# A gather pipeline paced by TensorE: pairs of indirect DMAs wait for products two groups in front and for their own group's

## The chip, the cores and the metric

The kernel runs on one core of one Trainium2 chip. The metric is the device time of one execution in microseconds, taken without the profiler; the kernel before has a median of 1033.82 us over 3 runs (1021.22 to 1034.26). A profile is a separate execution that the hardware profiler records.

## The reference

One message-passing layer of a graph network, with a residual and two layer norms. There are N = 6250 nodes with H = 128 features, E = 100000 edges sorted by destination, and 4 attributes per edge.

```python
msg_in = concatenate([x[src], x[dst], edge_attr])        # E x 260
h = silu(msg_in @ mW1 + mb1)                             # E x 128
messages = h @ mW2 + mb2
aggregated = segment_sum(messages, dst, N)               # N x 128
u = silu(concatenate([x, aggregated]) @ uW1 + ub1)
updated = u @ uW2 + ub2
x = layernorm(x + layer_norm(x + updated))
```

## The kernel before

**Tiling.** Edges are taken in tiles of 128 and in groups of 8 tiles (`G = 8`), so there are 98 groups (`NG`); the last one has 6 tiles. Since the first product is linear, it is split: `x[src] @ W1a` is a lookup in a table `tab_a` (one row of 128 floats per node, kept in DRAM), `x[dst] @ W1b + mb1` comes from a second table `tab_b`, and the attributes are multiplied directly. A first stage makes both tables: 13 batches of up to four node tiles are transposed and multiplied (L321, L328), copied (L344 for `tab_a`) and written to DRAM.

**One group g** passes through these steps:

- `fetch(g)` (L176 to L186): up to 8 indirect DMAs on GpSimd (POOL), one per tile, each gathering 128 rows of 512 bytes into `rows[g]`. Groups 0 to 4 (`RAW = 5`) gather rows of `x` itself, since the table isn't ready yet; from group 5 on they gather rows of `tab_a`.
- `load(g)` (L453): on the SyncE queue, the destinations (`near`), 80 rows of `tab_b` that cover the group's destinations (`mv`), and the attributes.
- `matrices(g)` (L464): two comparisons on VectorE (L468, L478) that make the 0/1 matrices "edge belongs to destination row", one for each direction.
- `before_rows(g)` (L493): 8 products on TensorE, `pre` (L500), which spread the destination rows and attributes over the edges. For a raw group, the gathered rows are transposed (L489, L491) and multiplied in as well (L502).
- `hidden(g)` (L507): VectorE adds the gathered rows and `pre` (L515), ScalarE applies SiLU into `h` (L516). Raw groups skip the add (L512).
- `sums(g)` (L518): one transpose (L522) and 8 products (L524) on TensorE sum `h` over the edges of each of 80 destinations, and VectorE adds the result into the batch's accumulator at an offset from a register (`add`, L545).

**Nodes.** Every 8 groups a batch of four node tiles is complete, for g = 8, 16, ..., 88, 94 and 97. `node_stage` (L627) then spreads its work over three groups: `node_u` (L562, L569, L570, L572) after `sums(8m)`, `node_y` (L578, L580, L582) one group later, `node_z` and `node_o` (L588 to L622) after a further group. The next batch's node loads, transposes and `tab_b` products (L328) are placed around the same groups.

**Order.** The order on each engine is the order in which the program writes the instructions; a framework only inserts semaphore waits for data and for buffers. In iteration g of the main loop (L652) the order is `fetch(g + 4)`, `load(g + 3)`, `hidden(g)`, `matrices(g + 2)`, `before_rows(g + 1)`, `sums(g)`, `add(g)`, node work. So TensorE has pre(g), sums(g-1), pre(g+1), sums(g) in turn. POOL has nothing but gathers after the first stage. The rows' pool has 6 buffers (`AHEAD + 2`), so the first gather of a group waits until the group six before has been read (for table groups, by L516); the other seven have no wait on a compute engine. A gather also waits for an older gather that used the same DMA semaphore.

Of the kernel before, what the change touches and what calls it, by code (L numbers as in the profile page):

```python
# [24 lines left out]
def kernel(  # L25
# [18 lines left out]
    nc = tc.nc  # L44
# [5 lines left out]
    G = 8  # L50
# [3 lines left out]
    W = 80  # L54
# [6 lines left out]
    RAW = 5  # L61
    NM = 4
# [23 lines left out]
    def tiles_of(g):  # L86
        return min(G, TI - g * G)
# [16 lines left out]
    start = ExitStack()  # L104
    first = start.enter_context(tc.tile_pool(name="first", bufs=1, side="right"))

    def wide():
        return ps.tile([P, G, P], F32, name="pre")

    def narrow():  # L110
        return ps1.tile([P, 2 * P], F32, name="pt")
# [60 lines left out]
    tab_b = dram.tile([NW, H], F32, name="tab_b")  # L172
    ea_d = dram.tile([ED, NG * GE], F32, name="ea_d")
    rows, bases, near = {}, {}, {}

    def fetch(g):  # L176
        if g >= NG:
            return
        rows[g] = gath.tile([P, G, H], F32, name="ga")
        for i in range(tiles_of(g)):  # L180
            nc.gpsimd.indirect_dma_start(  # L181
                out=rows[g][:, i, :],
                out_offset=None,
                in_=x if g < RAW else tab_a[:, :],
                in_offset=bass.IndirectOffsetOnAxis(ap=src_i[:, g, i : i + 1], axis=0),
            )  # L186

    for g in range(RAW - 1):
        fetch(g)
# [6 lines left out]
        ceil_i, pattern=[[BN * P, NB + 1], [0, G]], base=BN * P - W, channel_multiplier=0  # L196
    )
    fetch(RAW - 1)

    b1 = bcast("b1", mb1)  # L200
# [146 lines left out]
    def turned_first(k):  # L347
        pt = wide()
        if k < 2:
            turned_x(k, pt, node, name="xT", bufs=3)  # L350
        else:
            turned_x(k, pt, first, name="xT", bufs=2)
        return pt

    pt = {0: turned_first(0)}
# [25 lines left out]
    mv = []  # L381
# [80 lines left out]
    oh, pre, xg = {}, {}, {}  # L462
# [30 lines left out]
    def before_rows(g):  # L493
        if g >= NG:
            return
        raw = g < RAW
        pre[g] = wide()
        st = stbuf[g % NST].rearrange("k (i c) -> k i c", i=G)
        for i in range(tiles_of(g)):
            nc.tensor.matmul(pre[g][:, i, :], st[:, i, :], mv[g % NM], start=True, stop=not raw)  # L500
            if raw:
                nc.tensor.matmul(  # L502
                    pre[g][:, i, :], xg[g][:, i, :], w1[:, 0, :], start=False, stop=True
                )
        xg.pop(g, None)
# [12 lines left out]
    def sums(g):  # L518
        n = tiles_of(g)
        h, o = hbuf[g % 2], oh.pop(g)  # L520
        pt = narrow()
        nc.tensor.transpose(pt[0:1, P : P + W], deg_g[:, g : g + 1], ident[:W, :W])  # L522
        for i in range(n):
            nc.tensor.matmul(pt[:, :W], h[:, i, :], o[:, i, :], start=i == 0, stop=i == n - 1)  # L524
        return pt

    acc, deg = {}, {}
# [57 lines left out]
    def inverse(*parts):  # L585
        r = node.tile([P, 2, 2 * BN], F32, name="r")
        lo, hi = parts[0][0], parts[-1][1]
        nc.scalar.activation(r[:, 0, lo:hi], var[:, lo:hi, 1], AF.Sqrt, bias=eps)  # L588
        nc.vector.reciprocal(r[:, 0, lo:hi], r[:, 0, lo:hi])
        nc.vector.scalar_tensor_tensor(  # L590
            r[:, 1, lo:hi], var[:, lo:hi, 0], -1.0, r[:, 0, lo:hi], op0=OP.mult, op1=OP.mult
        )
        return r

    def scaled(to, v, r, lo, n):
        for i in range(n):
            nc.scalar.activation(  # L597
                to[:, i, :],
                v[:, i, :],
                AF.Identity,  # L600
                bias=r[:, 1, lo + i : lo + i + 1],
                scale=r[:, 0, lo + i : lo + i + 1],
            )
# [11 lines left out]
    def node_o(k, r):  # L615
        i0, n = batches[k]
        o = node.tile([P, BN, H], F32, name="o")
        scaled(o, z_sb.pop(k), r, BN, n)
        m = min(i0 + n, nf) - i0
        if m > 0:  # L620
            nc.sync.dma_start(
                out[i0 * P : (i0 + m) * P].rearrange("(i p) f -> p i f", p=P), o[:, :m]  # L622
            )
        if i0 + n > nf:
            nc.scalar.dma_start(out[nf * P :], o[: N - nf * P, nf - i0, :])
# [26 lines left out]
    for g in range(NG):  # L652
        if g == 2:
            weights()
        if g == 5:
            merged()
        if g == 6:
            checks(*lists)
            source_lists(1, SK)
            start.close()  # L660
        for c in range(1, NC):
            if g == max(1, c * EC // GE - 8):
                attributes(c)
            if g == max(1, c * EC // GE - 8) + 1:
                attribute_rows(c)
        if g + AHEAD >= RAW:
            fetch(g + AHEAD)
        if g < RAW:
            if g + 1 < RAW:
                turned_rows(g + 1)  # L670
            before_rows(g)
        load(g + LEAD)
        hidden(g)
        matrices(g + 2)
        if g + 1 >= RAW:
            before_rows(g + 1)
        if g == NG - 1:
            node_x(NB - 1)
        add(g, sums(g))
        node_stage(g)  # L680
    k = NB - 1
    n = batches[k][1]
# [6 lines left out]
    node_o(k - 1, r)  # L689
    r = inverse((BN, BN + n))  # L690
    node_o(k, r)
    edges.close()
    ub2_b, g_b, b_b = late["ub2"], late["g"], late["b"]

# [100 lines left out]
    with tc.If(bad > 0):  # L795
        with tc.tile_pool(name="all", bufs=1) as whole:
# [11 lines left out]
            with tc.tile_pool(name="turned", bufs=2, space=PSUM) as turned:  # L808
                for i in range(NT):
                    pt = turned.tile([P, P], F32, name="pt")  # L810
# [142 lines left out]
```

## Time and profile before

| | |
|---|---|
| Median of 3 runs (lowest, highest) | 1033.82 us (1021.22, 1034.26) |
| Profiled execution, and its span | 1463.32 us, 1461.5 us |
| Mean granted TensorE clock in it | 0.561 |
| First gather from `tab_a` (group 5) starts | 93.1 us |
| First gather of group 11 starts | 176.2 us |
| Last gather ends | 1392.6 us |
| DMA over the span | 110.01 MB, 75 GB/s mean |

The profiled execution is 41% longer than the median of the runs. PE is TensorE, PEld its weight load, DVE VectorE, ACT ScalarE, POOL GpSimd, SP SyncE. In a row of groups the columns are line, engine, operation, output and inputs, count, then busy time, mean ns of one, and the idle time of the engine just before, with what ended most of it. A row of the timeline has start, duration, engine, line, operation and count, and in brackets the idle time before it and its releaser. "remote" stands for a wait whose releaser the profile doesn't show, and "issue" for idle time in which the engine waited for nothing that the profile shows.

### The profile page before, as it was taken

The page shows a single profiled execution, that of the slowest core. Times are in us where ns is not written, and L with a number is a line of the kernel's source. Part 1 is how long each engine was busy: PE and PEld are TensorE (multiplying, and loading weights), DVE is VectorE, ACT ScalarE, POOL GpSimd, SP SyncE. Part 2 cuts the span into 40 slices and gives each one's busy share as a digit, 9 for nine tenths or more (in the row PEclk, how much of TensorE's full clock was granted, in tenths as well). Part 3 has the DMA queues.
Part 4 walks back from the last instruction along what each step waited for, and adds up shares of the span by engine and source line. Part 5 has one row for each costly group of instructions (what it writes and reads, how often), then busy time and mean ns, then how long its engine had stood idle before and what let it go on. Part 6 is the DMA issues. An engine that isn't in the chain of part 4 may idle for free.

```text
span 1461.5 us, 12138 instructions
## 1 busy us (share of the span) xinstructions
PE 885.3 (61%) x3858; PEld 777.7 (53%) x3858; DVE 451.3 (31%) x936; ACT 238.8 (16%) x338; POOL 739.3 (51%) x792
## 2 busy tenths in 40 slices
PE   2355766466456747554764764766764764764794
PEld 2355755464455645443763663664653763663683
DVE  0032332322322422412522422422422422422443
ACT  0010112111111201201201301211201201201213
POOL 7334555464554654564564565465564565465400
PEclk9987756556555555555555555555555555555555
DMA  6243313122222222221321321331331321322200
GB/s 165 61 117 92 94 58 87 54 83 63 78 79 61 84 68 77 74 77 41 96 84 47 100 81 51 87 92 52 93 92 46 91 86 52 88 65 64 85 26 19
DMA packets 83074, 110.01 MB, mean 75 GB/s; under 512 B 21084, under 2 KB 62160, under 8 KB 83002
## 3 DMA queue, kind: packets, MB, share of 16 engines
q1 hardware_dynamic: 54178, 55.97, 13.2%
q0 software_dynamic: 25024, 51.30, 12.6%
q10 hardware_dynamic: 3800, 1.88, 0.5%
q8 instruction: 33, 0.54, 0.1%
q14 instruction: 39, 0.32, 0.1%
HBM read 97.81 MB, written 11.27 MB: 75 GB/s over the span
## 4 chain that ended last, share of the span: by engine, by line
another core or an unknown queue 37%; PE 25%; DVE 16%; issue 12%; ACT 5%; DVEq 2%; DMA 1%; POOL 1%; ACTq 0%; SPq 0%
PE pt L524 12%; PE pre L500 4%; DVE ga L515 4%; DVE st L468 4%; ACT h L516 3%; DVE oh L478 2%; PE pn L569 2%; PE pn L570 2%; ACT pn L597 2%; DVE bn L556 1%; PE pn L328 1%; DVE var L557 1%; PE pre L328 1%; DVEq L515 1%
## 5 line engine op out<-in xcount | busy, mean ns | idle before, releaser
L181 POOL DMA_INDIRECT ga<-tab_a,src_i x742 | 699.9, 943 | 638.5 <-ACT h L516 372.1
L524 PE MATMUL pt<-oh,h 128*128 128x80 f32 x1564 | 348.1, 415 | 174.6 <-ACT h L516 156.8
L524 PEld LDWEIGHTS pt<-oh,h 128*128 128x128 f32 x1564 | 332.8, 323 | 194.9 <-ACT h L516 172.2
L500 PE MATMUL pre<-mv,st 84*128 84x128 f32 x1564 | 351.0, 409 | 23.1 <-issue 22.1
L500 PEld LDWEIGHTS pre<-mv,st 84*128 84x128 f32 x1564 | 332.4, 318 | 28.3 <-issue 27.0
L545 DVE TENSOR_TENSOR acc<-acc,pt 128x80 f32 x98 | 23.4, 238 | 733.1 <-remote 504.1
L516 ACT ACTIVATE h<-ga 128x1024 f32<-128x1024 f32 (+1 forms) x93 | 98.1, 1055 | 726.2 <-DVE ga L515 541.1
L522 PE MATMUL pt<-ident,deg_g 80*1 80x80 f32 x98 | 30.9, 315 | 191.6 <-DVE deg L545 191.6
L468 DVE TENSOR_SCALAR_CACHE_REDUCE st<-near,base_p 80x1024 f32<-80x1024 int32 x98 | 124.3, 1269 | 7.1 <-issue 5.2
L515 DVE TENSOR_TENSOR ga<-ga,pre 128x1024 f32<-128x1024 f32 (+1 forms) x93 | 113.2, 1217 | 26.8 <-issue 22.0
L522 PEld LDWEIGHTS pt<-ident,deg_g 80*1 80x1 f32 x98 | 10.7, 109 | 199.7 <-DVE deg L545 199.6
L478 DVE TENSOR_TENSOR oh<-w_row,rel 128x640 f32<-128x640 f32 x98 | 79.8, 814 | 0.0
L569 PE MATMUL pn<-acc,wc 128*128 128x512 f32 (+2 forms) x26 | 24.3, 1037 | 89.2 <-DVE acc L545 89.2
L569 PEld LDWEIGHTS pn<-acc,wc 128*128 128x128 f32 x26 | 6.9, 312 | 106.2 <-DVE acc L545 104.1
L181 POOL DMA_INDIRECT ga<-in_x_dram,src_i x40 | 37.9, 947 | 14.2 <-issue 11.7
L321 PE MATMUL pre<-ident,x 128*128 128x128 f32 x49 | 13.8, 434 | 43.6 <-issue 26.6
L321 PEld LDWEIGHTS pre<-ident,x 128*128 128x128 f32 x49 | 8.6, 216 | 47.5 <-issue 26.9
L328 PEld LDWEIGHTS pn<-w,xT 128*128 128x128 f32 x98 | 20.2, 305 | 25.6 <-ACT uT L572 22.7
L597 ACT ACTIVATE pn<-y,r 128x128 f32<-128x128 f32 x49 | 22.6, 461 | 65.6 <-DVE r L590 59.0
L344 DVE COPY ta<-pre 128x512 f32<-128x512 f32 (+2 forms) x13 | 8.6, 661 | 75.9 <-remote 42.3
L337 DVE TENSOR_TENSOR o<-pn,b 128x512 f32<-128x512 f32 (+2 forms) x13 | 8.6, 661 | 74.3 <-PE pn L328 63.1
L536 ACT COPY acc<-acc 128x256 f32<-128x256 f32 (+1 forms) x12 | 5.0, 413 | 159.8 <-DVE acc L545 155.8
(117 smaller groups left out, 532.8 us busy)
## 6 DMA issues: line engine op xcount, KB each, us to landing
near<-in_dst_dram SPq DMA_DIRECT2D x97, 320.0 KB
ga<-tab_a,src_i POOLq DMA_INDIRECT x742
mv<-tab_b SPq DMA_DIRECT2D x98, 40.0 KB
x<-in_x_dram SPq DMA_DIRECT2D x14, 256.0 KB
tab_a<-ta SPq DMA_DIRECT2D x11, 256.0 KB
tab_b<-o SPq DMA_DIRECT2D x11, 256.0 KB
out_dram<-o SPq DMA_DIRECT2D x11, 256.0 KB
st<-ea_d SPq DMA_DIRECT2D x98, 16.0 KB
```

What stands on the lines that cost most here:

```text
L181: nc.gpsimd.indirect_dma_start(out=rows[g][:, i, :], out_offset=None, in_=x if g < RAW else tab_a[:, :], in_offset=bass.IndirectOffsetOnAx ...
L328: nc.tensor.matmul(pm[:, i, :], xT[k][:, i * P : (i + 1) * P], w1[:, part, :], start=True, stop=True)
L468: nc.vector.tensor_scalar(stbuf[g % NST][:W], near.pop(g), base_p[:W, g : g + 1], 0.0, op0=OP.is_equal, op1=OP.add, accum_out=deg_g[:, g : ...
L478: nc.vector.tensor_tensor(oh[g][:, :n], w_row[:, None, :].to_broadcast([P, n, W]), rel[:, g, :n, None].to_broadcast([P, n, W]), op=OP.is_e ...
L500: nc.tensor.matmul(pre[g][:, i, :], st[:, i, :], mv[g % NM], start=True, stop=not raw)
L515: nc.vector.tensor_add(s[:, :n], s[:, :n], p[:, :n])
L516: nc.scalar.activation(h[:, :n], s[:, :n], AF.Silu)
L522: nc.tensor.transpose(pt[0:1, P : P + W], deg_g[:, g : g + 1], ident[:W, :W])
L524: nc.tensor.matmul(pt[:, :W], h[:, i, :], o[:, i, :], start=i == 0, stop=i == n - 1)
L569: nc.tensor.matmul(p, wc, acc[k][:, : n * P], start=False, stop=False)
L570: nc.tensor.matmul(p, bc_row, deg[k][:, : n * P], start=False, stop=True)
L597: nc.scalar.activation(to[:, i, :], v[:, i, :], AF.Identity, bias=r[:, 1, lo + i : lo + i + 1], scale=r[:, 0, lo + i : lo + i + 1],)
```

## The change

The gathers of groups 6 to 97 are remembered if their index i is even, and the products of TensorE are remembered by group and tile. After the main program each remembered gather gets a dependence on one product. Gathers 0 and 2 of group g wait for products 0 and 4 of `sums(g - 2)`; gathers 4 and 6 wait for products 0 and 4 of `before_rows(g)`, which is their own group's `pre`. Gathers 1, 3, 5 and 7 get no wait, but stand behind them on POOL. The order of instructions on all engines is unchanged. The products that are waited for signal their completion; the buffer's wait falls together with the new one.

```diff
@@ -172,18 +172,21 @@
     rows, bases, near = {}, {}, {}
+    steps, done = [], {}
 
     def fetch(g):
...
-            nc.gpsimd.indirect_dma_start(
+            ins = nc.gpsimd.indirect_dma_start(
...
             )
+            if g > RAW and i % 2 == 0:
+                steps.append((ins, g, i))
@@ -497,7 +500,9 @@
         for i in range(tiles_of(g)):
-            nc.tensor.matmul(pre[g][:, i, :], st[:, i, :], mv[g % NM], start=True, stop=not raw)
+            done["pre", g, i] = nc.tensor.matmul(
+                pre[g][:, i, :], st[:, i, :], mv[g % NM], start=True, stop=not raw
+            )
@@ -521,7 +526,9 @@
         for i in range(n):
-            nc.tensor.matmul(pt[:, :W], h[:, i, :], o[:, i, :], start=i == 0, stop=i == n - 1)
+            done["sum", g, i] = nc.tensor.matmul(
+                pt[:, :W], h[:, i, :], o[:, i, :], start=i == 0, stop=i == n - 1
+            )
@@ -689,6 +696,14 @@
+    for ins, g, i in steps:
+        after = done[("sum", g - 2, 2 * i) if i < G // 2 else ("pre", g, 2 * i - G)]
+        tc.add_manual_dep(
+            ins.ins,
+            after.ins.name,
+            mybir.DependencyInfo(mybir.DependencyClass.Sync, mybir.DependencyReason.DATA),
+            reason="pace",
+        )
```

## The prediction

> **What bounds the kernel now.** I read the page's engine totals and costliest groups, then the waits by total, then the timeline of a pair of groups and of the end, then that of the first groups.
>
> ```profile
> PE 885.3 (61%) x3858; PEld 777.7 (53%) x3858; DVE 451.3 (31%) x936; ACT 238.8 (16%) x338; POOL 739.3 (51%) x792
> ...
> L181 POOL DMA_INDIRECT ga<-tab_a,src_i x742 | 699.9, 943 | 638.5 <-ACT h L516 372.1
> ```
>
> 742 gathers from the table at 943 ns, and each is followed by 0.30 us in which POOL waits for nothing visible: start to start the timeline shows 1.249 us. All 782 gathers together cannot take less than 782 x 1.249 = 977 us.
>
> ```profile
> DVE acc L545 <- remote: 504.1, 35, 15.5
> POOL ga L181 <- ACT h L516: 372.1, 53, 15.6
> ```
>
> 35 stalls of L545 with no releaser named make up 504 us. The timeline shows one:
>
> ```profile
> 842.92 3.62 PE L524 MATMUL pt<-oh,h 128*128 128x80 f32 x16
> 846.34 3.70 PE L500 MATMUL pre<-mv,st 84*128 84x128 f32 x16
> ...
> 853.49 0.94 POOL L181 DMA_INDIRECT ga<-tab_a,src_i  x1 [0.30 <-issue]
> 854.73 0.94 POOL L181 DMA_INDIRECT ga<-tab_a,src_i  x1 [0.30 <-issue]
> 858.64 0.24 DVE L545 TENSOR_TENSOR acc<-acc,pt 128x80 f32 x1 [15.42 <-remote]
> ```
>
> TensorE's sums end at 846.5, but VectorE's add, which waits for them, starts at 858.6, 3 us after the last of 16 gathers in a row. POOL then waits 6 to 8 us for the next h. So a pair of groups takes about 26 us. Where no gather runs, the stall is gone:
>
> ```profile
> 1388.71 3.70 PE L500 MATMUL pre<-mv,st 84*128 84x128 f32 x16
> 1395.76 3.70 PE L500 MATMUL pre<-mv,st 84*128 84x128 f32 x16
> 1402.80 3.70 PE L500 MATMUL pre<-mv,st 84*128 84x128 f32 x16
> ```
>
> 7.05 us a group, with TensorE busy throughout at the granted clock of 0.5.
>
> **Which time counts.** The profiled execution took 1463.3 us (span 1461.5), the unprofiled runs have a median of 1033.8, 41% apart. 1033.8 leaves only 57 us over the 977 us of gathers, so at this period POOL can hardly ever wait in those runs: the 12 us stalls cannot be there. A sum supports it. The table's 13 steps come every 3.66 us once gathers pause (L344 at 64.06, 67.72), but one waited 28.7 us in the gather train before; undisturbed, the table would be ready some 28 us before 93, and the raw groups lose about 10 us of such waits. The gather for group 11, at 176.2 in the trace, then starts near 138 (an estimate). From there 694 gathers are left: 138 + 694 x 1.249 + about 25 for the last group = 1030. I take the runs to be POOL-bound, with TensorE behind at 7.05 us a group plus node work against POOL's 10.0.
>
> **What the Trainium skill says.** DMA: Bandwidth & Descriptors, section "Anatomy of one DMA": DMA engines wait on no semaphore; the wait is on the issuing sequencer. So a gather that waits holds all gathers behind it; the trace agrees in that POOL's idle 372 us lie before whole trains. Perfetto Trace Analysis, "Summary: the profiler window per engine type": a gather's bar ends with its descriptors, not its data; here the gather that ended at 855.67 had landed by 857.2, 1.5 us later. TensorE: Matmul & The Clock Gate, "The cost: per-tile semaphore tail": an increment costs about 26 ns.
>
> **The change part by part.** Instruction order on every engine is unchanged; the even gathers of groups 6 to 97 (367 of them) get TensorE's semaphore to wait for. Gather 0 of group g waits for the first product of sums(g-2), gather 2 for its fifth, gather 4 for the first of pre(g), gather 6 for its fifth. TensorE's order is pre(g-1), sums(g-2), pre(g). The buffer's wait, h(g-6), is implied.
>
> *Instructions*: POOL's semaphore wait is 17 ns and fits in the 0.30 us gap (already so at 848.40): nothing. Four more increments a group, 4 x 26 ns x 92 = 10 us by the skill's price, lie in TensorE's idle 3 us a group: nothing, 10 us without that cover.
>
> *Head start lost.* In the trace POOL gathers groups 6 to 10 while TensorE works on raw groups 0 to 4, and gather 11 waits for h(5):
>
> ```profile
> 170.08 2.00 PE L524 MATMUL pt<-oh,h 128*128 128x80 f32 x16
> ...
> 174.87 1.06 ACT L516 ACTIVATE h<-ga 128x1024 f32<-128x1024 f32 x1
> ...
> 176.20 0.94 POOL L181 DMA_INDIRECT ga<-tab_a,src_i  x1 [9.18 <-ACT h L516]
> ```
>
> After, group 6 itself waits for sums(4), whose first product ends about 170.6, 5.6 us before 176.2. Five groups (40 gathers, 50.0 us) that were hidden now come after it: 50.0 - 5.6 = +44 us, wherever the raw groups lie.
>
> *Ordinary groups.* After POOL's end of group g-2: landing 1.5, add 1.6 to h's start (840.07 to 841.65), h 1.06, first product 0.85, signals 0.2: 5.2 us. Gather 0 of group g would start 0.3 + 8 x 1.249 = 10.3 after the same moment: slack 5.1. The fifth product comes 1.7 later, slack 5.9; pre(g) follows, slack 6.3 and 7.1. No wait: 0 us.
>
> *Node stages*, every 8 groups, where TensorE is late. After sums(8m), L562 2.07, L569 and L570 4.15, a pause of 0.75 and L328 1.87 put 8.8 us before the next pre; one group later L578 and L580 put 3.8; after a third the next sums start 12.6 us after the last, since the add waits behind node work on VectorE (sums at 823.25 and 835.80).
>
> ```profile
> 800.29 2.08 PE L569 MATMUL pn<-acc,wc 128*128 128x512 f32 x2 [9.78 <-DVE acc L545]
> 802.30 2.07 PE L570 MATMUL pn<-deg,bc_row 1*128 1x512 f32 x2
> 805.15 2.08 PE L328 MATMUL pn<-w,xT 128*128 128x128 f32 x8 [0.78 <-ACT uT L572]
> ```
>
> Against slacks: pre 8.8 late - 6.3 = 2.5 us of POOL wait; next pre: 16.0 - 10 + 3.8 = 9.8 late - 6.3 - 2.5 = 1.0; then sums 9.6 late - 5.1 - 3.5 = 1.0. Together 4.5 us a stage; before, 50 us of rows ahead hid all of it. While POOL waits, rows come later too, but TensorE is later still. With the full clock, which the profile grants for 3.4 us inside some stages, the delays halve and nothing is left. Bounds 0 to 4.5; I take 3.5, near the slow end because the clock is mostly 0.5: 11 x 3.5 = +38 us (0 to 50).
>
> Sum: 1033.8 + 44 + 38 = **1116 us**. Own range 1075 to 1145: both ends of the stages, and 15 us for the start. Against the profiled execution the same sum would be 1463 + 82; but its stalls depend on gather trains, which the change cuts, so I forecast no profiled time.
>
> **Rivals.** (1) *Gathers are quicker unprofiled, TensorE bounds.* For: TensorE needs 7.05 + (8.8 + 3.8 + 5.5)/8 = 9.3 us a group, 93 x 9.3 = 865 from about 132, nearly the median too. Against: 943 ns is the same at every gather. At 1.0 us POOL has 8.0 a group, the slack shrinks by 2 a group and stages cost POOL 12 or so: (64 + 12 - 74) x 11 = about 22, with 5 at the start: 1060 (1034 to 1090). (2) *Faster: the trains do hold TensorE's semaphores back in unprofiled runs.* Place: L545 during 16-gather trains; price: the 6.2 us that POOL idles per pair of groups. Then (1034 - 138 - 25)/87 = 10.0 = 8 x + 3.1 gives x = 0.86 a gather; cutting trains to two frees the semaphores and TensorE's 9.3 bounds: 130 + 92 x 9.3 + 25 = 1011, less if denser work raises the clock (8.4: 928); I put 975. It decides once over 1.2 us a group (a third of 3.1, or 105 us) is regained, more than the losses above. Against: 1033.8 is explained without it. (3) *Each pair pays a semaphore delay*: if TensorE's increment shows only 1.4 us after the last landing, four waits a group may add 4 x 1.4 x 92 = 515: 1550. For: the profile's stalls; against: as for (2). The change taking no effect is excluded by the new waits in POOL's order.
>
> **How the numbers follow.** Likeliest case 64% (63 slower), (1) 15% (5 slower, 10 the same), (2) 14% (12 faster, 2 the same), (3) 7% slower; the likeliest's last 1% is the same. Faster by over 2% 0.12, same 0.13, slower 0.75; 2% is about what a measurement of this kernel tells from none. The range 1000 to 1160 holds the likeliest and (1), and a part of (2); left out are (3) and most of (2).
>
> **What would show it.** Right: gather 48 (the first of group 6) starts just after sums(4), not at 103; POOL's longest waits name PE, at L500 and L524, and lie in the groups after 8m; an undisturbed group takes 10 us. Wrong: POOL waits in ordinary groups, or L545's waits for remote go while gathers still run, with the unprofiled time below 1013: then the stalls were real in those runs.

## The result, and the profile after

The changed kernel takes 1096.76 us (median of 4 runs, 1092.13 to 1097.53), the kernel before 1027.52 beside it: a ratio of 1.0667 [1.0563, 1.077], 69.2 us slower. The forecast was 1116, from 1033.8. The profile of the changed kernel shows an execution of 1096.36 us (span 1094.6), so here the profile and the runs agree.

The kernel before has two times, about 1025 us in some batches of runs (runs taken together on one chip) and about 1470 in others (one chip gave both in two batches), so every comparison below is with the kernel before in the same batch, and the result stands in a batch of the first kind, the quicker one, while the profile shown ahead of the prediction is of the second kind.

So the trace to compare with is not the one of 1463 us, but one of the kernel before that was recorded at 1030.08 us (span 1028.3; first run below). The page of the changed kernel, costliest POOL group and engine totals:

```profile
PE 837.8 (77%) x3858; PEld 743.5 (68%) x3858; DVE 451.4 (41%) x936; ACT 239.2 (22%) x338; POOL 739.7 (68%) x792
...
L182 POOL DMA_INDIRECT ga<-tab_a,src_i x742 | 700.3, 944 | 308.1 <-issue 178.6
```

The gather costs what it did, 944 ns. What grew is the idle time before it: 308.1 us, where the kernel before has 241.8. Its waits in total (engine, line, releaser: us in all, times, longest):

```profile
POOL ga L182 <- issue: 190.0, 624, 0.3
...
POOL ga L182 <- PE pt L529: 90.0, 55, 45.2
...
POOL ga L182 <- PE pre L503: 22.1, 44, 2.1
```

"issue" is the 0.30 us after every gather, which the kernel before has too. The loss names PE. One wait of 45.2 us is half of the line for the sums (L529, which was L524 before); the waits for `pre` (L503, before L500) are at most 2.1. No wait for ACT's h is left. The timeline shows where the long one lies:

```profile
108.89 1.95 PE L529 MATMUL pt<-oh,h 128*128 128x80 f32 x16
...
109.55 0.94 POOL L182 DMA_INDIRECT ga<-tab_a,src_i  x1 [45.17 <-PE pt L529]
```

That is gather 48, the first of group 6, held until the first product of `sums(4)` is out. Over the 0.30 us of every gather it loses 44.9 us; the rest of the new waits sum to 37.2 us. Of these 1.8 lie at group 7, whose `pre` comes late on TensorE behind the transposes that make the next source indices (L164), and the rest in groups behind node stages. The last full stage's part, POOL alone:

```profile
997.37 0.94 POOL L182 DMA_INDIRECT ga<-tab_a,src_i  x1 [1.29 <-PE pre L503]
...
1002.72 0.94 POOL L182 DMA_INDIRECT ga<-tab_a,src_i  x1 [0.66 <-PE pt L529]
...
1015.69 0.94 POOL L182 DMA_INDIRECT ga<-tab_a,src_i  x1 [3.28 <-PE pt L529]
```

They are gathers of groups 91, 92 and 93, after `node_stage` began behind `sums(88)`; less 0.30 each they cost 1.0, 0.4 and 3.0. The largest is explained on TensorE, which is idle for 5.63 us, waiting for `h`, before the sums (second row) that gather 0 of group 93 waits for:

```profile
1001.73 3.70 PE L529 MATMUL pt<-oh,h 128*128 128x80 f32 x16 [1.51 <-ACT h L521]
...
1014.70 3.71 PE L529 MATMUL pt<-oh,h 128*128 128x80 f32 x16 [5.63 <-ACT h L521]
```

Two rounds of sums lie 13.0 us apart, where POOL needs 10.0 for a group. VectorE shows why `h` is late: between one add (L552) and the sum of rows and `pre` that makes the next `h` (L520) stands the work on the nodes, with a wait for ScalarE in it:

```profile
1005.47 0.24 DVE L552 TENSOR_TENSOR acc<-acc,pt 128x80 f32 x1 [3.00 <-PE pt L529]
...
1008.25 0.70 DVE L616 TENSOR_TENSOR pn<-pn,g_b 128x512 f32<-128x512 f32 x1 [2.09 <-ACT pn L604]
...
1012.33 1.22 DVE L520 TENSOR_TENSOR ga<-ga,pre 128x1024 f32<-128x1024 f32 x1 [0.19 <-issue]
```

Between stages nothing is lost: of POOL's waits from 287 to 350 us, six groups, none is over 0.3 us; these rows show the last number, the longest:

```profile
POOL ga L182 <- issue: 12.8, 42, 0.3
...
POOL ga L182 <- PE pre L503: 0.3, 1, 0.3
POOL ga L182 <- PE pt L529: 0.3, 1, 0.3
```

### The profile page after: what moved, and what is told of

The parts are those of the page before. It is cut to its first block, busy times and chain, and to the rows that moved or that the text cites. A ratio compares the mean times of both kernels' runs of the same rounds, so it can differ in the third digit from the quotient of the medians.

```text
span 1094.6 us, 12413 instructions
## 1 busy us (share of the span) xinstructions
PE 837.8 (77%) x3858; PEld 743.5 (68%) x3858; DVE 451.4 (41%) x936; ACT 239.2 (22%) x338; POOL 739.7 (68%) x792
## 4 chain that ended last, share of the span: by engine, by line
PE 35%; POOL 14%; issue 14%; DMA 13%; DVE 10%; ACT 7%; DVEq 1%; ACTq 0%; SPq 0%; POOLq 0%
PE pt L529 19%; POOL ga L182 14%; DMA ga<-tab_a,src_i 12%; PE pre L503 7%; ACT h L521 5%; DVE ga L520 5%; ACT pn L604 1%; PE pn L587 1%; PE pn L585 1%; DVE bn L563 1%; PE pn L569 1%; PE pn L576 1%; PE pn L577 1%; PE pre L507 1%; DVE var L564 1%
## 5 line engine op out<-in xcount | busy, mean ns | idle before, releaser
L182 POOL DMA_INDIRECT ga<-tab_a,src_i x742 | 700.3, 944 | 308.1 <-issue 178.6
L529 PE MATMUL pt<-oh,h 128*128 128x80 f32 x1564 | 339.8, 407 | 189.3 <-ACT h L521 185.0
L529 PEld LDWEIGHTS pt<-oh,h 128*128 128x128 f32 x1564 | 321.8, 313 | 221.3 <-ACT h L521 214.5
L503 PE MATMUL pre<-mv,st 84*128 84x128 f32 x1564 | 340.0, 402 | 10.2 <-DVE xg L494 9.3
L503 PEld LDWEIGHTS pre<-mv,st 84*128 84x128 f32 x1564 | 323.8, 312 | 12.3 <-DVE xg L494 9.7
L520 DVE TENSOR_TENSOR ga<-ga,pre 128x1024 f32<-128x1024 f32 (+1 forms) x93 | 113.2, 1217 | 139.5 <-DMA ga<-tab_a,src_i 134.7
L552 DVE TENSOR_TENSOR acc<-acc,pt 128x80 f32 x98 | 23.4, 239 | 306.1 <-PE pt L529 299.6
L587 PEld LDWEIGHTS pn<-u,uT 128*128 128x128 f32 x98 | 21.6, 323 | 15.3 <-issue 15.3
L569 PE MATMUL pn<-xT,u 128*128 128x512 f32 (+2 forms) x26 | 24.3, 1039 | 4.2 <-DVE z L619 4.2
L589 DVE TENSOR_TENSOR y<-pn,x 128x512 f32<-128x512 f32 (+2 forms) x13 | 8.6, 660 | 42.3 <-PE pn L587 42.3
L587 PE MATMUL pn<-u,uT 128*128 128x128 f32 x98 | 25.4, 439 | 0.0
L331 PE MATMUL pn<-w,xT 128*128 128x128 f32 x98 | 17.7, 333 | 9.3 <-ACT uT L579 8.6
L331 PE MATMUL pre<-w,xT 128*128 128x128 f32 x98 | 17.6, 339 | 6.8 <-ACT xT L326 6.8
L585 PE MATMUL pn<-ub_row,ones 1*128 1x512 f32 (+2 forms) x26 | 21.8, 934 | 0.6 <-ACT uT L579 0.6
```

Source lines behind the costliest of these rows:

```text
L182: ins = nc.gpsimd.indirect_dma_start(out=rows[g][:, i, :], out_offset=None, in_=x if g < RAW else tab_a[:, :], in_offset=bass.IndirectOffs ...
L331: nc.tensor.matmul(pm[:, i, :], xT[k][:, i * P : (i + 1) * P], w1[:, part, :], start=True, stop=True)
L503: done["pre", g, i] = nc.tensor.matmul(pre[g][:, i, :], st[:, i, :], mv[g % NM], start=True, stop=not raw)
L520: nc.vector.tensor_add(s[:, :n], s[:, :n], p[:, :n])
L529: done["sum", g, i] = nc.tensor.matmul(pt[:, :W], h[:, i, :], o[:, i, :], start=i == 0, stop=i == n - 1)
L569: nc.tensor.matmul(pu[k], u1[:, 0, :], xT.pop(k)[:, : n * P], start=True, stop=False)
```

## The experiments

**Theory: start and stages.** POOL is the bound at 1.249 us a gather; the change costs the head start at group 6 and a few us in every node stage, and nothing else. **Rival A** (the prediction's second): trains of gathers (gathers in a row without a pause) hold TensorE's semaphores back, also without the profiler, and the pairs pay off by ending that. **Rival B** (its third): every waiting pair has a price of its own, whatever it waits for.

**The kernel before, profiled again** (no edit).

> The kernel before, unchanged, profiled a second time. If the stalls of VectorE's add behind trains of gathers belong to one disturbed execution and not to the program, the profiled span is near the median of the unprofiled runs (1020 to 1040 us), no wait for a hidden releaser is over a few us, and POOL waits for less than about 60 us in all. If the stalls belong to the program under the profiler, the span is near 1460 us again.

It took 1030.08 us under the profiler, 1022.62 beside it without. So the profiler does not add 41%. Its costliest POOL group, and its waits by total:

```profile
L181 POOL DMA_INDIRECT ga<-tab_a,src_i x742 | 700.1, 944 | 241.8 <-issue 215.8
```

```profile
DVE acc L545 <- PE pt L524: 329.3, 97, 5.8
POOL ga L181 <- issue: 227.2, 746, 0.3
...
POOL ga L181 <- ACT h L516: 18.4, 9, 7.2
```

VectorE's add (L545), which waited 504.1 us for a remote releaser in the profile of 1463, waits only for the sums themselves, at most 5.8. POOL waits 18.4 us for h, nine times; less 0.30 each that is 15.7. The gather that the change holds back longest:

```profile
64.88 0.94 POOL L181 DMA_INDIRECT ga<-tab_a,src_i  x1 [0.30 <-issue]
```

Group 6 starts at 64.88 here and at 109.55 after the change, 44.7 later. The last gather ends at 996.4 here and at 1062.8 after, 66.4 later, and both kernels need 32 us more to their end. The sum closes: 44.9 + 37.2 - 15.7 = 66.4. That is the bookkeeping of one engine; which waits are causes is for the next runs to show. The 15.7 vanish since a gather that comes 45 us later finds its buffer free.

**One wait alone.**

```diff
-            if g > RAW and i % 2 == 0:
+            if g == RAW + 1 and i == 0:
```

> Only gather 0 of group 6 waits, for the first product of sums(4). Beside a kernel before of about 1028, where VectorE's add has no waits for a remote releaser: start theory, 1057 (44.6 at group 6 less the 16 that the kernel before waits at groups 12 to 17), that is 40 below the changed kernel, whose node stages make up the rest; rival (the start is free, all of the 69 comes from the later waits): 1028. Beside a kernel before of about 1470: 1.02 times it, as twice measured.

Measured: 1056.38 against 1022.56, ratio 1.0289 [1.0214, 1.0365]. POOL's waits:

```profile
POOL ga L182 <- issue: 228.5, 750, 0.3
...
POOL ga L182 <- PE pt L529: 44.3, 1, 44.3
```

One new wait, and of those for h none over 0.3 us any more. One semaphore wait at one gather makes 33.8 of the 69 us by the medians; by the traces the last gather ends 29.0 later than in the kernel before (at 1025.4), and 44.0 less 15.7 is 28.3, near the 29 that was expected. The rival that the start is free falls. The same kernel ran in two other batches, in which the kernel before took 1468.41 and 1472.91:

> Of the 367 new waits only one is left: the first gather of group 6 waits for the first product of sums(4). Theory (lost head start): POOL resumes at 109.5 us instead of 64.9 and nothing gives the 45 us back, except that the 15 us which the kernel before waits for h(6), h(10) and h(11) no longer arise; POOL ends near 1026 us, and the time is about 1027 + 30 = 1057 (1050 to 1064). Rival (every paced wait costs POOL something, 69 us over 367 waits = 0.19 us each): 1028, the same as before.

> Of all new waits only one stays: gather 0 of group 6 waits for the first product of sums(4). Theory: this alone loses the head start of five groups, 44.6 at group 6, and some 16 come back, because the kernel before waits that long itself at groups 12 to 17 and this one would not: 1028 + 29 = 1057 beside 1028, with POOL's gather 48 at about 109 and no further wait of over 3 us. Beside 1468 it gave +24 in the last batch, and should again give 20 to 30. Rival (the start costs nothing, the later waits cost all): no difference from the kernel before.

Measured: 1492.68, ratio 1.0186 [1.0107, 1.0265], and 1497.81, ratio 1.0193 [1.0102, 1.0283]. The absolute time of the first expectation was for the other kind of batch; the difference, +24 and +25, lies within what was expected. The lost head start costs in both kinds of batch.

**All waits one group further back.**

```diff
-        after = done[("sum", g - 2, 2 * i) if i < G // 2 else ("pre", g, 2 * i - G)]
+        after = done[("sum", g - 3, 2 * i) if i < G // 2 else ("pre", g - 1, 2 * i - G)]
```

> All waits one group further back: sums(g-3) and pre(g-1). Beside a kernel before of about 1022: theory, the 10 us more of slack hides the node stages whole (the changed kernel's 37 become 0 to 4) and group 6 waits for sums(3), 8 to 10 us before sums(4): 44.6 - 9 = 35 at group 6, less the 16 that the kernel before waits itself: 1022 + 19 to 23, that is 1041 to 1050, below the 1056 of one wait alone although all 367 waits are there. Rival (each of the 367 waits has a price of its own, whatever it waits for): above 1056 and near the changed kernel's 1092 to 1097. Beside a kernel before of about 1470: 0.885 times it, as twice measured.

Measured: 1050.42 against 1026.83, ratio 1.0234 [1.0167, 1.0301]. The waits of over 1 us, in the timeline of POOL:

```profile
100.94 0.94 POOL L182 DMA_INDIRECT ga<-tab_a,src_i  x1 [36.56 <-PE pt L529]
...
128.31 0.94 POOL L182 DMA_INDIRECT ga<-tab_a,src_i  x1 [2.15 <-PE pre L503]
...
189.24 0.94 POOL L182 DMA_INDIRECT ga<-tab_a,src_i  x1 [6.32 <-PE pt L529]
```

Less 0.30 each they cost 36.3 us at group 6, which starts 8.6 us earlier than with the change, then 1.8 at group 8 and 6.0 at group 14, which follows the first node stage. As I read it, TensorE is still catching up with the raw groups there. From 190 us on not one of some 330 waits costs anything. With 10 us more slack the later stages are free, as the theory says; the 7.8 us at groups 8 and 14 are more than was expected (0 to 4). By the medians the kernel is 23.6 us slower, where 19 to 23 were expected. Rival B falls: with all 367 waits the ratio is no higher than that of one wait (1.0289), and most of the waits cost nothing.

**The other kind of batch.** Beside a kernel before of 1468.41, three variants with many waits; the first is the edit just shown, the other two pace only from group 12 and from group 54 on:

```diff
-            if g > RAW and i % 2 == 0:
+            if g > 11 and i % 2 == 0:
```

```diff
-            if g > RAW and i % 2 == 0:
+            if g > 53 and i % 2 == 0:
```

> All 367 waits are kept, each on the same product of one group earlier (sums(g-3) and pre(g-1)). Theory: the slack grows by 10 us, which is more than the waits in the node stages need, so these 35 us go; the start only regains 7 us (sums(3) at 102 us): POOL ends near 1021 and the time is 1050 to 1058. Rivals (a cost of every wait, or of spreading gathers among TensorE's work): as the change, 1097.

> The pacing begins with group 12, so that the start is as in the kernel before. Theory: the head start is only lost later, since gather 0 of group 12 (132 us in the kernel before) must wait for sums(10) (174 us there), and group 13 for sums(11) (190 us); then the stage waits as in the change: 1095 to 1105, no better than the change. Rival (the cost lies in the first groups): 1027 + 37 - 15 = 1050. Rival (0.19 us a wait, 343 waits): 1092.

> The pacing begins with group 54. Theory: TensorE has caught up with POOL by then except for some 16 us (group 54 is gathered at 559.8 us and sums(52) begins at 575.8 us in the kernel before), and stages from group 64 on cost about 19 us: 1027 + 35 = 1062 (1052 to 1070). Rival (0.19 us a wait, 175 waits): 1060, so this run does not tell the two apart by its time; the trace should show one wait of about 16 us at group 54 and none in ordinary groups.

Measured: 1303.24, ratio 0.8849 [0.8776, 0.8923]; 1299.57, ratio 0.8884 [0.8805, 0.8962]; 1383.39, ratio 0.9456 [0.9373, 0.9539]. All three expectations missed, and in sign: they were made for a kernel before of about 1027 and said slower. A second batch, beside 1472.91, had the changed kernel itself and two variants, the last with the waits three groups further back:

```diff
-        after = done[("sum", g - 2, 2 * i) if i < G // 2 else ("pre", g, 2 * i - G)]
+        after = done[("sum", g - 5, 2 * i) if i < G // 2 else ("pre", g - 3, 2 * i - G)]
```

> The changed kernel once more, in one batch with three variants of it. Theory (start and stages): where the kernel before takes about 1028 beside it, 1097 (44.6 at group 6, some 37 in the groups of the node stages, less 16 that the kernel before waits itself). Rival (trains hold TensorE's semaphores back): where the kernel before takes some 1468 beside it, as it did beside the last batch, VectorE's add waits for a remote releaser in long gather trains; trains of two would end that, and the changed kernel would be faster than the kernel before, at or below the 1299.6 of the variant that paced from group 12 on; 1250 to 1300. The first theory alone would put it at 1468 + 69 = 1537 there.

> All waits one group further back: gathers 0 and 2 of group g wait for sums(g-3), 4 and 6 for pre(g-1). Theory: each group has 10 us more slack, so the node stages cost nothing, and group 6 waits for sums(3), some 10 us before sums(4): 44.6 - 10 - 16 = 19 to 27 over the kernel before, 1047 to 1055 beside 1028; most of the distance to the changed kernel (1097) comes back. Rival (each pair pays a semaphore's delay whatever it waits for): about as slow as the changed kernel. Beside 1468 it gave 1303 in the last batch and should do so again.

> All waits three groups further back: gathers 0 and 2 of group g wait for sums(g-5), 4 and 6 for pre(g-3). Theory: the node stages cost nothing, and group 6 waits for sums(1), so that the loss at the start shrinks by about 10 a group to 10 to 20, of which up to 16 are those that the kernel before waits anyway: 1026 to 1040 beside 1028, no gain over the kernel before, because 782 gathers at 1.249 remain. Beside 1468: rows run up to 50 us ahead again and trains grow to 16 where TensorE is late, so between 1303 and 1468 if the length of a train decides; below 1303 if the lead does not matter and only the pairs do.

> All waits three groups further back: sums(g-5) and pre(g-3). Beside a kernel before of about 1025: theory, the stages cost nothing, and group 6 waits for sums(1), 16 to 18 us before sums(3), for which the last variant waited 36.3 there: 18 to 20 at group 6, less the 16 that the kernel before waits itself, so 2 to 10 over the kernel before, 1027 to 1035. Rival (the waits have a price of their own): 1045 or more, as the last variant, since as many waits are there. Beside a kernel before of about 1470: 0.887 times it, as measured once.

Measured: the changed kernel 1300.12, ratio 0.8793 [0.8676, 0.8909]; one group further back 1293.3, ratio 0.8831 [0.8743, 0.8918]; three groups 1298.28, ratio 0.8868 [0.8791, 0.8945], and again 1305.24 beside 1476.21, ratio 0.8919 [0.8813, 0.9024]. Here the change makes the kernel 12% faster, which is what Rival A says and the theory alone (1537) does not. Two kernels of this batch by their waits, first the one with a single wait:

```profile
DVE acc L552 <- remote: 530.5, 34, 22.9
POOL ga L182 <- ACT h L521: 391.3, 49, 14.8
```

and the one with all waits one group further back:

```profile
DVE acc L552 <- remote: 245.3, 23, 15.7
POOL ga L182 <- issue: 201.5, 648, 1.6
...
POOL ga L182 <- PE pt L529: 118.4, 51, 39.0
POOL ga L182 <- PE pre L503: 88.8, 39, 7.7
```

The remote stalls of the add halve. POOL's 391.3 us for h are gone; it waits 207.2 for PE (39.0 of them at the start) and 46.6 for a remote releaser.

Where does the delay arise? The trace of 1463 keeps events of TensorE's semaphore. For the add at 858.64 that the prediction shows, the sums ended at 846.54, but two events of that semaphore stand at 858.62 and 858.78 and none between 845.91 and those; before all 34 adds that come over 4 us after their sums, such an event is recorded within 0.06 us of the add's start. By these events it is the increment that comes late, and not VectorE that notices it late. (This trace keeps 310 events for 352 increments, the one of 1030 us all of them.)

I counted trains, gathers with no more than 0.5 us between them, and those in which sums end whose add comes over 4 us later. In the profile of 1463 these are all 32 trains of 16 and none of the 22 trains of 8; in the kernel with the waits one group further back, 15 of 17 trains of 12, both of 14, 2 of the 11 of 10, none of the 29 of 8 and 2 of the 40 of 2 to 6. Over all ten traces of this kind, of the trains in which sums end, they are 7 of 264 trains of 8, 25 of 73 of 10, 74 of 95 of 12, all 18 of 14 and all 116 of 16. So the stall goes with the length of a train, and pairs that wait break most long trains. That gathers hold the increments back is the reading that fits, since pausing them shrinks the stalls; but a stalled VectorE may in turn lengthen a train, as POOL goes on until its buffers are used up, and no run pauses the gathers without a wait for TensorE. The order of cause and effect within a train is not shown.

The gain goes with the number of paced groups, not with how far back they wait: 44 groups (from 54 on) gain 85.0 us, 1.9 each; 86 groups (from 12 on) gain 168.8, 2.0 each; and 2, 3 or 5 groups of lead all end at 0.88 to 0.89. That they stay near 1300 rather than near 1050 goes with the 245.3 us that remain; 17 of the 28 late adds of that trace lie at trains of 12 and 14.

Left open: how three groups further back stands where the kernel before takes 1025 (both of its batches were of the other kind; the theory says 1027 to 1035; if so, it would lose little there and win 11% here), what a batch of the second kind has that the other lacks, and by what path an increment of TensorE is held back.

## Why the prediction was right

**The bound.** POOL at 1.249 us a gather and no stalls of the add: right for the runs that count. But the reason that the prediction gave was half wrong. It read "41% apart" as profiled against unprofiled; they are two kinds of batch, and for the second kind, where the runs take 1470, "the 12 us stalls cannot be there" does not hold. What was sound is the arithmetic: with 782 gathers, 1033.8 us leave no room for them. The prediction chose the right one of the two kinds from the time alone. That matters for the sign: in the other kind the same change is 12% faster.

**Head start, +44.** Measured 44.9 at group 6, in a place that the prediction had only from a trace in which group 11 came 61 us later (176.2 against 115.3). The count (five groups, 50.0 us, less the time by which `sums(4)` comes before group 11) survived, as it said, "wherever the raw groups lie": that time was 5.6 us there and is 6.0 here. The Trainium skill, DMA: Bandwidth & Descriptors, section "Anatomy of one DMA", says that the wait for a semaphore is on the issuing sequencer, so one waiting gather holds every later one; the run with one wait agrees, 33.8 us slower by one wait.

**Ordinary groups, 0.** Right: slacks of 5.1 to 7.1 us were enough everywhere between the stages.

**Instructions, 0.** Right. TensorE: Matmul & The Clock Gate, section "The cost: per-tile semaphore tail", prices an increment at about 26 ns where each small matmul of a packed array signals; the prediction took that price over to these products, 10 us in all. No run isolates it, and none shows it: eight products of `pre` take a median 3.70 us in the traces of both kernels, though two of them signal after the change, and with 367 waits kept and the slack raised POOL loses nothing after 190 us.

**Node stages, +38.** Measured 37.2, or 35.4 without the 1.8 at group 7: 3.2 us a stage, where 3.5 was forecast. The parts came otherwise. Forecast were 2.5 at the first `pre`, 1.0 at the next and 1.0 at the sums; the means over eleven stages are 0.2, 0.4 and 2.4 (and 0.1 at the sums between). The first `pre` was put too late: from the end of `sums(8m)` to it the prediction counted 8.8 us at the clock of 0.5, and the trace has 5.3 to 6.4 in the nine stages in which the full clock is granted for 2.7 to 4.0 us of that stretch, and 8.1 and 7.3 after `sums(64)` and `sums(88)`, where it is not; only these two have a wait at the first `pre`. So the reason for going near the slow end, a clock that is mostly 0.5, was wrong at this place. The total held because in the prediction's own working the waits follow one another: what POOL has not lost at `pre` it loses at the sums (9.6 - 5.1 is 4.5 without any earlier wait; where its 9.6 comes from, the prediction does not show). These come 12.6 us after the last by the prediction and 13.0 in the trace, because `h` and the add stand behind node work on VectorE. Stages differ: 8.4 us after `sums(64)`, none after `sums(32)` and `sums(72)`.

**The term that was missed.** The sum was 82.3 from its base, the medians give 69.2. The kernel before itself waits 15.7 us for h (mostly at groups 12, 16 and 17), and these waits end when group 6 is late; so the start costs about 29 net and not 44. The prediction's step "the gather for group 11 then starts near 138 ... 138 + 694 x 1.249 + about 25 = 1030" hid it. In the trace it starts at 115.3; the waits are 15.2 from there, and the end after the last gather takes 32, not 25. 23 us too late a start and 22 us left out cancelled, so that the sum met the median by luck, through two errors.

**The rivals.** (1) Quicker gathers: no, 0.94 and 0.30 us in every trace. (2) Trains hold semaphores: not in the runs of the comparison; in the other kind of batch the change gains as it said, with a ratio of 0.88 where it had put 975/1034 = 0.94. It had the mechanism's place (L545) and its direction right. (3) A price for each pair: refuted by the run with all waits one group further back.

## What to carry to other kernels

A pacing wait costs what it takes from work that runs ahead, and it is paid once, at the first group where the lead is lost, plus wherever the slack is smaller than the consumer's largest irregularity; so set the distance from the latest stage, not from the ordinary group. The loss at the start is smaller by what the kernel would have waited later anyway. Where stalls go with long trains of transfers, the same waits can win more than they cost, so measure in each kind of run that occurs. If a profile and the runs are far apart, don't put it down to the profiler: record the same kernel once more before reading its waits. A sum that meets the measured total is checked only when its start and its end are checked too.

## What the runs showed of the hardware

An unchanged program had two times, 1013.66 to 1034.26 us and 1454.82 to 1481.62 us. In each of five batches with seven runs of it all runs were of one kind; the first profile, 1463.32, stands beside runs of 1021 to 1034, and whether it was taken together with them is not on record. The two traces with granted clocks of 0.561 and 0.562 took 1463 and 1030 us, so the clock does not make the difference, though over all runs it was somewhat lower in the slower kind (0.542 to 0.576 against 0.562 to 0.616). The gather took the same 0.94 us.

What differed most is that VectorE's add started up to 12 us after the end of TensorE's sums, about 3 us after the last of 16 gathers, when an increment of TensorE's semaphore is recorded; with no gather running it started at once, and in traces of the quicker kind it did so in trains of hundreds of gathers. Eight waits of other instructions in the trace of 1463, 145.0 us together, also have no releaser that the profile shows, and the first gather from the table starts 38 us later there. Pausing the gathers every few us took back 165 to 180 us of some 445. Of the trains in which sums ended, 7 of 264 trains of 8 delayed the add, 74 of 95 of 12, and all 134 of 14 and 16.
